# Asking for the first groups' places, features and B rows inside the first stage of a graph layer

## The chip, the cores and the metric

The kernel runs on one core of one Trainium2 chip. The metric is device time in microseconds (us). A core has TensorE (PE, with its weight loads shown apart as PEld), VectorE (DVE), ScalarE (ACT), GpSimd (POOL) and SyncE (SP). In this kernel SP computes nothing: it issues most of the DMAs, in the order of the program, and POOL issues the indirect DMAs that gather rows. Each engine has its own list of instructions and works through it in order.

## The reference

One layer of a graph network with a pre-norm and a gated update. There are N = 12,500 nodes with 128 features and E = 400,000 edges with 32 features, sorted by their destination.

```
h   = relu(layernorm(x))                                   # 12500 x 128
m   = relu(concat(h[src], h[dst], ea) @ w1 + b1) @ w2 + b2 # one row per edge
agg = segment_sum(m, dst)                                  # 12500 x 128
gi  = agg @ w_ih + b_ih ;  gh = h @ w_hh + b_hh            # three parts each: r, z, n
r = sigmoid(gi_r + gh_r) ; z = sigmoid(gi_z + gh_z) ; n = tanh(gi_n + r * gh_n)
out = x + (1 - z) * n + z * h
```

## The kernel before

w1 is cut into three parts. The part for the source gives a table A = h @ w1a, the part for the destination a table B = h @ w1b + b1, and both tables lie in the chip's memory (DRAM) with one row of 512 bytes for each node. The part for the edge features is applied with each group of edges.

**First stage** (lines 354 to 488). The nodes are taken in 14 batches (0 to 13): batch 0 has 4 tiles of 128 nodes, batches 1 to 11 have 8, batch 12 has 5, and batch 13 has the last 84 nodes. A loop over q = 0 to 28 works on chunks of up to 4 tiles, so most batches are two chunks. For each chunk ACT normalises (line 263), PE turns the tiles (line 450), DVE or ACT copies the turned tiles into hT_all, which stays in on-chip memory (line 468), PE multiplies them with w1a (line 487), and ACT copies the product into a buffer asb (line 458). When a batch is complete, SP stores asb to A (line 482). There are two asb buffers: batch b + 2 may be written into asb only when the store of batch b has landed. In the same loop SP asks for the later batches of x (line 375), for three rows of source numbers per q from q = 4 on (line 423, tile `at`, 60 rows in all), and stores the first three pieces of B (lines 258 and 260). Meanwhile POOL gathers the rows of x for edge groups 0 to 8.

**Edges** (from line 490 on). The edges form 391 groups of 8 tiles of 128 edges (group 0 has 5 tiles), and the loop at line 1075 takes half a group at a time (u = 0 to 781). A group needs:

- L, a tile of 128 rows. The lower 64 rows take the places of the edges' destinations (a row of whole numbers, repeated over 32 partitions for each half) and DVE turns these into a one-hot matrix in place (onehot_T, line 586). The upper 64 rows are the edge features. `fetch(q)` (line 567) asks for L for groups 2q and 2q + 1: two DMAs of 256 KB on SP, one from dstP (line 574) and one from eaP (line 577). There are three L buffers.
- RW, 40 rows of B around the group's destinations in two overlapping windows of 32, with the edge part of w1 below them. `window_rows(k)` (line 600) asks for the windows of group k: two DMAs of 16 KB on SP at an address that SP has read into a register. At the first group of a block of 14, SP loads the block's 14 addresses with one instruction (line 606). There are four RW buffers.
- the rows of the sources. Groups 0 to 8 gather x itself (before A exists), normalise it and multiply it with w1a. Sixty groups are brought by hand: 28 by ACT and 27 by DVE, which copy columns of hT_all, and 5 by SP, which issues one small DMA per row of A. The other 322 groups are gathered from A by POOL (line 163), eight indirect DMAs for each group and 2,576 in all, into a ring of 11 buffers G.

PE multiplies L with RW (line 683), the result and the gathered rows are added and rectified into RB (DVE line 713, or ACT line 725 for the raw and the turned groups), and PE sums RB over destinations with a second one-hot matrix (line 739). Every 14 groups a block of 512 nodes goes through the gated update (`node`, line 790), and the last block through `last_node` (line 857).

The DVE and ACT groups brought by hand are collected in buffers HE_dve and HE_act, two of each, from a pool `pj` that is open from the start. The L buffers belong to a pool `p3` that is opened when the first stage's pool is closed and takes its place in memory. Before the loop over the groups, after the first stage, SP's list holds `dst_tile(1)` (line 1033), `fetch(0)` to `fetch(2)`, and `window_rows(0)` to `window_rows(3)`. Inside the loop come `window_rows(k + 4)` and `fetch(k // 2 + 3)`.

In the built program, SP's DMAs (other than the single rows of the five SP groups) take eight completion semaphores in turn, and each of them waits until the DMA that had its semaphore before, the eighth before it, has landed.

Of the kernel before, what the change touches and what calls it, by code (L numbers as in the profile page):

```python
# [9 lines left out]
F32 = mybir.dt.float32  # L10
F16 = mybir.dt.float16
I32 = mybir.dt.int32
U8 = mybir.dt.uint8
U16 = mybir.dt.uint16
BF16 = mybir.dt.bfloat16
ET = mybir.EngineType
# [4 lines left out]
N, E, D, DE = 12500, 400000, 128, 32  # L21
# [5 lines left out]
NP = T // PAIR + 1  # L27
NU = 2 * NP

V = 32  # L30
SHIFT = 8
# [32 lines left out]
def tile_gnn(ctx: ExitStack, tc: tile.TileContext, x, src, srcT, dstT, dstP, eaT, eaP, w1, b1, w2T, b2,  # L64
# [238 lines left out]
    def setup(pool):  # L303
# [45 lines left out]
        yield  # L349
        place(0)  # L350

    st_all = const.tile([128, NT, 2], F32, name="st_all")
    nc.vector.memset(st_all[:, NFULL, :], 0.0)
    with tc.tile_pool(name="pp", bufs=3) as pp:
        bats = [(sum(BAT[:b]), n) for b, n in enumerate(BAT)]
        xs = {}

        def PB(b):
            return 128 if bats[b][0] < NFULL else N - NFULL * 128

        def nodes(t, i0, n, P):
            return t[i0 * 128:i0 * 128 + n * P, :].rearrange("(p i) f -> p i f", p=P)


        def columns(b, c, e):
            i0, n = bats[b]
            t = hT_all[:, i0 * 128:i0 * 128 + n * PB(b)].rearrange("f (p i) -> f i p", i=n)
            return t[:, c:e, :]

        def load(b):  # L370
            if b < len(bats):
                i0, n = bats[b]
                P = PB(b)
                xs[b] = pp.tile([128, 8, D], F32, name="xs", bufs=5)
                nc.sync.dma_start(xs[b][:P, :n, :], nodes(x, i0, n, P))

        mvs, asb = {}, {}

        def stat(b):
            if b < len(bats):  # L380
                i0, n = bats[b]
                mvs[b] = bn(pp, lambda j: xs[b][:PB(b), j, :], PB(b), n)

        def sqr(b):
            if b < len(bats):
                mvs[b] = bn_sqrt(pp, mvs[b], PB(b), bats[b][1])

        def fin(b):
            if b < len(bats):
                i0, n = bats[b]  # L390
                bn_fin(pp, st_all[:, i0:i0 + n, :], mvs.pop(b), PB(b), n)

        for b in range(5):
            load(b)
        w1b = const.tile([128, D], F32, name="w1b")
        nc.sync.dma_start(w1b, w1[128:256, :])
        wih_s = const.tile([128, 3 * D], F32, name="wih_s")
        nc.sync.dma_start(wih_s, wih)
        whh_s = const.tile([128, 3 * D], F32, name="whh_s")
        nc.sync.dma_start(whh_s, whh)  # L400
        w2T_s = const.tile([128, D], F32, name="w2T_s")
        nc.sync.dma_start(w2T_s, w2T)
        b2_s = const.tile([128, 1], F32, name="b2_s")
        nc.sync.dma_start(b2_s, b2.rearrange("(f o) -> f o", o=1))
        row = lambda v: v.rearrange("(o f) -> o f", o=1)
        nc.sync.dma_start(brow[32:33, 0:384], row(bih))
        nc.sync.dma_start(brow[32:33, 384:512], row(bhh)[:, 256:384])
        nc.sync.dma_start(brow[33:34, 0:256], row(bhh)[:, 0:256])
        nc.sync.dma_start(b1b, row(b1).to_broadcast([128, D]))
        for r in RW:  # L410
            for a in range(2):
                nc.sync.dma_start(r[64 + 32 * a:96 + 32 * a, a, :], w1[256:288, :])

        indices(1)
        nc.sync.dma_start(base_d, dstT[0:1, SUP0::PAIR])
        dst_tile(0)
        rows_left = list(range(NJ))

        def at_row():
            if rows_left:  # L420
                r = rows_left.pop(0)
                t0 = tiles(by_hand[r])[0]
                nc.sync.dma_start(at[r:r + 1, :], row(src[t0 * 128:(t0 + PAIR) * 128]))

        stat(0)
        sqr(0)
        fin(0)
        stat(1)
        sqr(1)
        chunks = [(b, c) for b, (i0, n) in enumerate(bats) for c in range(0, n, 4)]  # L430

        def chunk(q):
            b, c = chunks[q]
            i0, n = bats[b]
            return b, i0, c, min(n, c + 4), PB(b), (i0 + c) * 128

        pts, pas = {}, {}
        NC = len(chunks)
        setting = setup(pp)
        for q in range(NC + 3):  # L440
            if q < NC:
                b, i0, c, e, P, n0 = chunk(q)
                if c == 0:
                    stat(b + 2)
                    fin(b + 1)
            if 1 <= q <= NC:
                b, i0, c, e, P, n0 = chunk(q - 1)
                pts[q - 1] = SEGB[q % 2]
                for j in range(c, e):
                    nc.tensor.transpose(pts[q - 1][:, (j - c) * P:(j - c + 1) * P],  # L450
                                        xs[b][:P, j, :], ident[:P, :P])
                if e == bats[b][1]:
                    load(b + 5)
            if q >= 3:
                b, i0, c, e, P, n0 = chunk(q - 3)
                if c == 0:
                    asb[b] = pp.tile([128, 8, D], F32, name="asb", bufs=2)
                nc.scalar.copy(asb[b][:P, c:e, :], pas.pop(q - 3)[:P, :e - c, :])
            if q < NC:
                b, i0, c, e, P, n0 = chunk(q)  # L460
                for j in range(c, e):
                    relu_norm(xs[b][:P, j, :], xs[b][:P, j, :], st_all[:P, i0 + j, :])
                if e == bats[b][1]:
                    sqr(b + 2)
            if 1 <= q <= NC:
                b, i0, c, e, P, n0 = chunk(q - 1)
                copy = nc.scalar.copy if q % 4 == 0 else nc.vector.tensor_copy
                copy(columns(b, c, e), pts.pop(q - 1)[:, :(e - c) * P].rearrange(
                    "f (i p) -> f i p", i=e - c))
            if q >= 4:  # L470
                for _ in range(3):
                    at_row()
            if q >= 6:
                next(setting, None)
            if q in (6, 8, 10):
                batch_product(q // 2 - 3, pp, "bt", 1)
            if q in (7, 9, 11):
                batch_store(q // 2 - 3)
            if q >= 3:
                b, i0, c, e, P, n0 = chunk(q - 3)  # L480
                if e == bats[b][1]:
                    nc.sync.dma_start(nodes(A, i0, e, P), asb[b][:P, :e, :])
            if 2 <= q <= NC + 1:
                b, i0, c, e, P, n0 = chunk(q - 2)
                pas[q - 2] = ps2.tile([128, PAIR, D], F32, name="pre")
                for j in range(c, e):
                    nc.tensor.matmul(pas[q - 2][:P, j - c, :], columns(b, j, j + 1)[:, 0, :],
                                     w1a, start=True, stop=True)
# [72 lines left out]
        nc.vector.tensor_copy(flag, f[:, 6:7])  # L561


    Ls, OH, RT, HE, SEG = ({} for _ in range(5))
    hand = {}

    def fetch(q):
        if q * QP >= NP:
            return
        n = min(QP, NP - q * QP)  # L570
        c = slice(q * QP * 512, (q * QP + n) * 512)
        Ls[q] = p3.tile([128, QP * 512], F32, name="L")
        p = dstP[:, c]
        nc.sync.dma_start(
            Ls[q].bitcast(I32)[:2 * V, :n * 512],
            bass.AP(tensor=p.tensor, offset=p.offset, ap=[list(p.ap[0]), [0, V], [1, n * 512]]))
        nc.sync.dma_start(Ls[q][2 * V:, :n * 512], eaP[:, c])

    def onehot_T(k):
        if k >= NP:  # L580
# [8 lines left out]
                                    accum_out=dlast[:2 * V, n:n + 1])  # L589


    bases = {}

    def block(k):
        return max(b for b in range(NB) if BLOCKS[b][0] <= k)

    def slot(b, i):
        return i // 2 if b < NB - 1 else (BP - BLOCKS[b][1]) // 2 + i // 2

    def window_rows(k):  # L600
        if k >= NP:
            return
        b = block(k)
        k0, n, _ = BLOCKS[b]
        if k == k0:
            _, vals = nc.values_load_multi_w_load_instructions(
                base_i[0:1, b, 0:n], engines=[ET.SP], min_val=0, max_val=4 * D * LAST,
                skip_runtime_bounds_check_because="clamped above")
            for i, v in enumerate(vals):
                bases[k + i] = v  # L610
        v = bases.pop(k)
        for a in range(2):
            nc.sync.dma_start(RW[k % 4].bitcast(U8)[V * a:V * (a + 1), a, :],
                              B_bytes[bass.ds(v + 4 * D * SHIFT * a, 4 * D * V)].rearrange(
                                  "(p f) -> p f", p=V))

    def onehot(k):
        if k >= NP or (k % 2 and k > 1):
# [412 lines left out]

    gathers(0)
    dst_tile(1)
    for q in range(3):
        fetch(q)
    for k in range(4):
        window_rows(k)


    def stages(u):  # L1040
# [248 lines left out]
```

## Time and profile before

| what | value |
|---|---|
| median of 3 runs | 3385.01 us (3376.61 to 3388.27) |
| the profiled execution | 3383.87 us |
| its span, first to last instruction | 3382.1 us |
| PE, DVE, ACT, POOL busy | 71%, 65%, 91%, 75% of the span |
| mean granted TensorE clock | 0.795 |

Busy time leaves out what an engine spends on issuing: POOL is shown busy for about 0.94 us of each gather and idle for the 0.30 us that it takes to go on to the next. In the timeline a row gives start, duration, engine, line, operation, what is written and read, how many instructions were merged (x3), and in brackets the idle time before the first and what ended it. SPq is SP's queue: a row is the time of issuing, not of the transfer. When several rows of SP are merged, the duration runs from the first issue to the end of the last and holds the waits between them. What ended a wait is inferred from semaphores. Since the semaphores of DMAs are used in turn, the DMA named can be a later user of the same semaphore.

### The profile page before, as it was taken

Reading aid. Unit: us, or ns where it says so; the run is one execution under the profiler, and the core shown is the slowest. Engines: PE = TensorE matmul, PEld = TensorE weight load, DVE = VectorE, ACT = ScalarE, POOL = GpSimd, SP = SyncE. Lnnn points to the kernel's source line nnn. Section 1 sums busy time; section 2 is a strip of 40 time slices with the busy share of each in tenths; the row PEclk is TensorE's granted clock in tenths of the full one; section 3 lists DMA queues with packets and bytes.
Section 4 is the critical chain, followed back from the end, with each engine's and each line's share of the span. In section 5 each row is a group of like instructions: output and inputs, shape, how many; then the busy total and the mean of one; then the engine's idle time right before and its main releaser. Section 6 shows DMA issues by size and latency. Waiting matters only on the chain. (4 is left out here: it accounts for less than half of the span.)

```text
span 3382.1 us, 93395 instructions
## 1 busy us (share of the span) xinstructions
PE 2400.4 (71%) x13113; PEld 1554.8 (46%) x13113; DVE 2213.6 (65%) x16274; ACT 3081.1 (91%) x29057; POOL 2542.8 (75%) x2654
## 2 busy tenths in 40 slices
PE   7567766776677677668776777677667767766767
PEld 6444444444444444445444444444444444444445
DVE  8566666766666666666667766666656666666665
ACT  7599899999999998998999999999889998988975
POOL 7777777777777777777777777777777777777775
PEclk9778777887888777877877878787777787778778
DMA  6433444444444444444444444444444444343332
GB/s 215 104 92 84 95 99 101 99 97 103 96 95 99 97 98 95 99 104 97 96 98 97 98 95 105 97 99 98 95 98 96 100 95 99 94 96 94 92 94 67
DMA packets 196737, 335.77 MB, mean 99 GB/s; under 512 B 69445, under 2 KB 118148, under 8 KB 196112
## 3 DMA queue, kind: packets, MB, share of 16 engines
q0 software_dynamic: 84640, 173.51, 23.0%
q1 hardware_dynamic: 111327, 156.18, 17.8%
q14 instruction: 517, 4.23, 0.4%
q8 instruction: 109, 1.79, 0.2%
q10 hardware_dynamic: 144, 0.07, 0.0%
HBM read 309.25 MB, written 20.24 MB: 97 GB/s over the span
## 5 line engine op out<-in xcount | busy, mean ns | idle before, releaser
L163 POOL DMA_INDIRECT G<-A,src_i x2576 | 2475.8, 961 | 790.4 <-issue 761.2
L979 ACT COPY HE_act<-hT_all 128x4 uint8 x28672 | 2889.0, 189 | 52.9 <-issue 29.1
L986 DVE SCALAR_TENSOR_TENSOR both<-hT_all 128x4 uint16 x13824 | 1174.3, 154 | 930.3 <-issue 925.6
L683 PE MATMUL pre<-RW,L 128*128 128x256 f32 x3128 | 1136.1, 489 | 461.3 <-DMA RW<-B 237.7
L683 PEld LDWEIGHTS pre<-RW,L 128*128 128x128 f32 x3128 | 662.8, 237 | 736.8 <-issue 420.2
L739 PE MATMUL seg<-RB,OH 128*32 128x129 f32 x6250 | 592.7, 319 | 244.2 <-DVE RB L713 211.9
L739 PEld LDWEIGHTS seg<-RB,OH 128*32 128x32 f32 x6250 | 328.0, 123 | 590.7 <-DVE RB L713 310.1
L713 DVE CUSTOM_DVE_ANT_0 RB<-pre,G 128x1024 f32<-128x1024 f32 x323 | 391.1, 1211 | 70.9 <-DMA G<-A,src_i 56.5
L586 DVE TENSOR_SCALAR L<-L,node_of 64x512 f32<-64x512 int32 x382 | 185.9, 487 | 62.2 <-DMA L<-in_dstP 59.9
L725 ACT ACTIVATE RB<-pre 128x1024 f32<-128x1024 f32 x64 | 65.0, 1016 | 91.0 <-PE pre L694 91.0
L633 DVE TENSOR_TENSOR OH<-dloc,seg 128x512 f32<-128x512 f16 (+1 forms) x198 | 132.3, 669 | 0.0
L765 PE MATMUL nd<-spot,sums 128*128 128x40 f32 x782 | 119.6, 326 | 3.6 <-DVE sums L748 3.6
L765 PEld LDWEIGHTS nd<-spot,sums 128*128 128x128 f32 x782 | 115.5, 237 | 12.7 <-issue 8.8
L991 DVE COPY HE_dve<-both 128x512 uint8<-128x512 uint8 x216 | 97.6, 452 | 7.4
L244 PE MATMUL nd<-w1b,hT_all 128*128 128x128 f32 x224 | 49.4, 368 | 73.1 <-DVE xb L850 73.1
L734 PE MATMUL seg<-zrow 1*128 1x129 bf16 x196 | 45.5, 232 | 78.1 <-DVE OH L633 78.0
L694 PEld LDWEIGHTS pre<-w1a,HE_dve 128*128 128x128 f32 x432 | 89.1, 255 | 12.4
L694 PEld LDWEIGHTS pre<-w1a,HE_act 128*128 128x128 f32 x448 | 85.9, 238 | 11.0
L694 PE MATMUL pre<-w1a,HE_dve 128*128 128x128 f32 x432 | 85.4, 333 | 0.0
L694 PE MATMUL pre<-w1a,HE_act 128*128 128x128 f32 x448 | 83.7, 319 | 0.0
L163 POOL DMA_INDIRECT G<-in_x,src_i x69 | 65.6, 950 | 21.9 <-issue 20.7
L244 PEld LDWEIGHTS nd<-w1b,hT_all 128*128 128x128 f32 x224 | 35.2, 231 | 85.5 <-DVE xb L850 80.0
(177 smaller groups left out, 1346.2 us busy)
## 6 DMA issues: line engine op xcount, KB each, us to landing
G_sp<-A SPq DMA_DIRECT2D x5120, 0.5 KB
L<-in_dstP SPq DMA_DIRECT2D x195, 256.0 KB
L<-in_eaP SPq DMA_DIRECT2D x195, 256.0 KB
G<-A,src_i POOLq DMA_INDIRECT x2576, 2.5
RW<-B SPq DMA_DIRECT2D x782, 16.0 KB
xb<-in_x SPq DMA_DIRECT2D x26, 256.0 KB
out<-xb SPq DMA_DIRECT2D x26, 256.0 KB
xs<-in_x SPq DMA_DIRECT2D x11, 512.0 KB
```

The lines of the kernel that those rows point to most:

```text
L163: fetched = nc.gpsimd.indirect_dma_start(out=G[k][:, j, a, :], out_offset=None, in_=table, in_offset=bass.IndirectOffsetOnAxis(ap=src_i[c] ...
L244: nc.tensor.matmul(pm[:m, i:i + D], hT_all[:, n0 + i:n0 + i + m], w1b, start=True, stop=True)
L586: nc.vector.tensor_scalar(o, i, node_of[:, k:k + 1], None, op0=ALU.is_equal)
L633: nc.vector.tensor_tensor(p, dloc[:, e0:e1, None].to_broadcast(shape), row[:, None, :].to_broadcast(shape), op=ALU.is_equal)
L683: nc.tensor.matmul(p[:, 2 * i:2 * i + 2, :], Ls[k // QP][:, c0:c0 + 128], RW[k % 4], start=True, stop=not raw)
L694: nc.tensor.matmul(p[:, 2 * i + a, :], cols, w1a, start=False, stop=n + 1 == len(l) or l[n + 1][1] != j)
L713: made = nc.vector._custom_dve(TENSOR_ADD_SAT, out=o, in0=p, in1=G[k].rearrange("p j a f -> p (j a) f")[:, c, :], s0=float("inf"), s1=0.0)
L739: nc.tensor.matmul(p[r0:r0 + V, :D + 1], OH[k][:, a * GRP + j, :], RB[k % 2][:, 2 * j + a, :D + 1], start=False, stop=all(b != a for _, _, ...
L765: nc.tensor.matmul(p[:, bass.ds(offs[i], V + SHIFT)], sums[:, slot(b, i), :D], spot[:, i % 2, :], start=False, stop=i == len(offs) - 1)
L979: nc.scalar.copy(he[:, e * 4:e * 4 + 4], column(v))
L986: nc.vector.scalar_tensor_tensor(both[:, (e0 % PIECE + i) // 2, :], column(vals[i + 1]), 256.0, column(vals[i]), op0=ALU.mult, op1=ALU.add)
L991: nc.vector.tensor_copy(he[:, p0 * 4:(p0 + PIECE) * 4].rearrange("p (n c b) -> p n c b", c=2, b=4), both.bitcast(U8).rearrange("p n (b c) ...
```

## The change

`fetch` and `window_rows` are defined before the first stage, and their first calls are moved into it. The addresses and the windows of groups 0 to 3 are asked for at q = 16, and L for groups 0 and 1, 2 and 3, 4 and 5 at q = 18, 20 and 22. The first three L tiles no longer come from the pool `p3` but are the first HE_dve, the second HE_dve and the first HE_act buffer. The functions are otherwise the same, and the calls after the first stage are gone. The loop over groups is not changed, so its `fetch(3)`, `fetch(4)` and `fetch(5)` now take L buffers that nobody has used before.

```diff
+    Ls = {}
+
+    def fetch(q):
+        if q * QP >= NP:
+            return
+        n = min(QP, NP - q * QP)
+        c = slice(q * QP * 512, (q * QP + n) * 512)
+        if q < 3:
+            Ls[q] = pj.tile([128, QP * 512], F32, name="HE_dve" if q < 2 else "HE_act")
+        else:
+            Ls[q] = p3.tile([128, QP * 512], F32, name="L")
+        p = dstP[:, c]
+        nc.sync.dma_start(
+            Ls[q].bitcast(I32)[:2 * V, :n * 512],
+            bass.AP(tensor=p.tensor, offset=p.offset, ap=[list(p.ap[0]), [0, V], [1, n * 512]]))
+        nc.sync.dma_start(Ls[q][2 * V:, :n * 512], eaP[:, c])
...
+    def window_rows(k):
...
+        if k == k0:
+            _, vals = nc.values_load_multi_w_load_instructions(
+                base_i[0:1, b, 0:n], engines=[ET.SP], min_val=0, max_val=4 * D * LAST,
+                skip_runtime_bounds_check_because="clamped above")
...
+        for a in range(2):
+            nc.sync.dma_start(RW[k % 4].bitcast(U8)[V * a:V * (a + 1), a, :],
...
@@ -476,6 +515,11 @@
                 batch_product(q // 2 - 3, pp, "bt", 1)
             if q in (7, 9, 11):
                 batch_store(q // 2 - 3)
+            if q == 16:
+                for k in range(4):
+                    window_rows(k)
+            if q in (18, 20, 22):
+                fetch((18, 20, 22).index(q))
             if q >= 3:
                 b, i0, c, e, P, n0 = chunk(q - 3)
                 if e == bats[b][1]:
...
     gathers(0)
     dst_tile(1)
-    for q in range(3):
-        fetch(q)
-    for k in range(4):
-        window_rows(k)
```

More of the change, by code (lines that the diff above doesn't have):

```diff
@@ L350, in setup, with block @@
         place(0)
+    Ls = {}
[13 more added lines that the diff above has]
+        nc.sync.dma_start(Ls[q][2 * V:, :n * 512], eaP[:, c])
+    bases = {}
+    def block(k):
+        return max(b for b in range(NB) if BLOCKS[b][0] <= k)
+    def window_rows(k):
+        if k >= NP:
+            return
+        b = block(k)
+        k0, n, _ = BLOCKS[b]
+        if k == k0:
+            _, vals = nc.values_load_multi_w_load_instructions(
+                base_i[0:1, b, 0:n], engines=[ET.SP], min_val=0, max_val=4 * D * LAST,
+                skip_runtime_bounds_check_because="clamped above")
+            for i, v in enumerate(vals):
+                bases[k + i] = v
+        v = bases.pop(k)
+        for a in range(2):
+            nc.sync.dma_start(RW[k % 4].bitcast(U8)[V * a:V * (a + 1), a, :],
+                              B_bytes[bass.ds(v + 4 * D * SHIFT * a, 4 * D * V)].rearrange(
+                                  "(p f) -> p f", p=V))
     st_all = const.tile([128, NT, 2], F32, name="st_all")
@@ L561, in check_windows @@
         nc.vector.tensor_copy(flag, f[:, 6:7])
-    Ls, OH, RT, HE, SEG = ({} for _ in range(5))
+    OH, RT, HE, SEG = ({} for _ in range(4))
     hand = {}
[L567 to L577, printed above, removed]
     def onehot_T(k):
@@ L589, in onehot_T @@
                                     accum_out=dlast[:2 * V, n:n + 1])
-    bases = {}
-    def block(k):
-        return max(b for b in range(NB) if BLOCKS[b][0] <= k)
     def slot(b, i):
         return i // 2 if b < NB - 1 else (BP - BLOCKS[b][1]) // 2 + i // 2
[L600 to L615, printed above, removed]
     def onehot(k):
```

## The prediction

> **What bounds the kernel now.** I read the page first, then what POOL waited for, then the timeline of POOL, then what DVE waited for in three stretches, then the first 130 us queue by queue. By busy time ACT looks like the bound, but the groups show that POOL is:
>
> ```profile
> span 3382.1 us, 93395 instructions
> L163 POOL DMA_INDIRECT G<-A,src_i x2576 | 2475.8, 961 | 790.4 <-issue 761.2
> ```
>
> The waits of POOL from 93 us to the end, and its timeline at the start of the A gathers, at its one later stop, and at its last gather:
>
> ```profile
> POOL G L163 <- issue: 761.2, 2496, 0.3
> POOL G L163 <- PE misc L666: 3.3, 4, 2.3
> ...
> 88.71 0.94 POOL L163 DMA_INDIRECT G<-in_x,src_i  x1 [0.30 <-issue]
> 92.84 0.94 POOL L163 DMA_INDIRECT G<-A,src_i  x1 [3.18 <-DMA L<-in_dstP]
> ...
> 121.57 0.94 POOL L163 DMA_INDIRECT G<-A,src_i  x1 [0.30 <-issue]
> 124.86 0.94 POOL L163 DMA_INDIRECT G<-A,src_i  x1 [2.34 <-PE misc L666]
> ...
> 3354.97 0.94 POOL L163 DMA_INDIRECT G<-A,src_i  x1 [0.30 <-issue]
> ```
>
> From 92.84 to 3354.97 POOL issues one gather after another. The only real stop is 2.34 us at 124.86, for a G buffer that a raw group still held. All else is the 0.3 us behind every gather. Whether the rest of the kernel has to follow POOL is told by the addition that uses the gathered rows (DVE, line 713), asked from 0 to 2250 us and from 2250 to 3225 us:
>
> ```profile
> L713 DVE CUSTOM_DVE_ANT_0 RB<-pre,G x212: 1204/1212/1226, 203.6 to 2249.2; 128x1024 f32<-128x1024 f32 x106
>   PE pre L683: 7.9, 8
> ...
> L713 DVE CUSTOM_DVE_ANT_0 RB<-pre,G x97: 1204/1217/1226, 2249.2 to 3220.2; 128x1024 f32<-128x1024 f32 x97
>   DMA G<-A,src_i: 56.5, 27
> ```
>
> The first use comes at 203.6, 111 us after POOL's first A gather. Up to 2249 the addition never waits for rows: ACT, DVE and PE start late and catch up. From there to 3220 it waits 27 times for rows that have only just been asked for. So the end follows POOL: the start of the A gathers, 2,576 gathers, and the last groups (3354.97 to 3382.1). Time saved for ACT, DVE or PE in the first 2200 us only makes them catch up sooner, while time lost by POOL is lost for good.
>
> **What the change aims at.** DVE and PE at the seam of the two stages:
>
> ```profile
> 91.14 1.10 PE L666 MATMUL misc<-ident,G 128*128 128x128 f32 x3 [2.44 <-ACT G L263]
> 100.32 0.48 DVE L586 TENSOR_SCALAR L<-L,node_of 64x512 f32<-64x512 int32 x1 [9.76 <-DMA L<-in_dstP]
> 118.39 1.19 PE L683 MATMUL pre<-RW,L 128*128 128x256 f32 x2 [11.73 <-DMA RW<-B]
> ```
>
> DVE stands 9.76 us for L, and the first product comes at 118.39, though the first raw tiles were turned by 92.24. Both waits go. But by the paragraph above, this is worth only what POOL gains: its stop at 124.86 falls away, since that buffer will be free earlier. That is 2.34 less the usual 0.30, or 2.04 us.
>
> **What the moved DMAs displace.** SP's queue from q = 16 on, as it stands before:
>
> ```profile
> 62.76 0.87 SPq L423 DMA_DIRECT2D at<-in_src  x3
> 66.01 0.32 SPq L375 DMA_DIRECT2D xs<-in_x  x1
> 66.37 0.85 SPq L423 DMA_DIRECT2D at<-in_src  x3
> 67.31 0.37 SPq L482 DMA_DIRECT2D A<-asb  x1
> ...
> 76.86 0.37 SPq L482 DMA_DIRECT2D A<-asb  x1
> ...
> 81.62 8.06 SPq L482 DMA_DIRECT2D A<-asb  x4
> ...
> 90.21 0.66 SPq L574 DMA_DIRECT2D L<-in_dstP  x1
> ...
> 91.65 0.57 SPq L574 DMA_DIRECT2D L<-in_dstP  x1
> ...
> 93.02 0.55 SPq L574 DMA_DIRECT2D L<-in_dstP  x1
> ...
> 93.61 4.96 SPq L577 DMA_DIRECT2D L<-in_eaP  x1
> ...
> 100.40 1.86 SPq L613 DMA_DIRECT2D RW<-B  x4
> ```
>
> The stores of batches 7 and 9 are issued at 67.31 and 76.86, and the row of four is batches 10 to 13. POOL's first A gather needs all of them landed: the last issue ends at 89.68 and the gather starts at 92.84, 3.2 us later. Now an L fetch, its landing and what stands behind it:
>
> ```profile
> SPq L613 <- DMA L<-in_dstP: 13.5, 2, 7.7
> ...
> 108.22 0.32 SPq L613 DMA_DIRECT2D RW<-B  x1
> ...
> 116.75 0.32 SPq L613 DMA_DIRECT2D RW<-B  x1
> ...
> 303.75 0.58 SPq L574 DMA_DIRECT2D L<-in_dstP  x1
> ...
> 312.81 0.33 SPq L507 DMA_DIRECT2D stats<-st_all  x1
> ```
>
> The windows issued at 108.22 and 116.75 are the eighth DMAs after the fetches of 91.65 and 93.02, so these are the landings of the second and third places tile. The first landed by 100.32, when DVE's wait ended. One after the other they take 10.1, 7.9 and 8.5 us. A lone fetch of 303.75 held up its eighth successor until 312.81, so it took 9.1 us. And the first windows, issued at 100.40, end PE's wait only at 118.39: they landed when the third L did, some 18 us after their issue. So an L fetch is slow, the fetches follow one another, and a DMA behind them in SP's queue is complete only after them.
>
> The Trainium skill, page "DMA: Bandwidth & Descriptors", section "Anatomy of one DMA", fits a DMA issued by GpSimd with 2.0 us plus its bytes over 436,000 per us; carried over to 256 KB that is an estimate of 2.6 us, nothing on SP would be held up, and the sum would be the gain of 2.04 us alone, 3381.8 us. The trace's 9 to 10 us speak against it. Section "Rules for kernel authors" of that page says that an outermost dimension of size c confines a DMA to at most c engines; the places fetch has an outermost dimension of 2, so by that rule the A stores too, which need all engines, wait behind it.
>
> I take 10.5 us from the issue of a places DMA to the landing of its pair: 10.1, and some for the eaP half, issued behind it. SP's list in the new order, step by step:
>
> - q = 16. The three rows end at 63.63. The load of the 14 addresses takes 1.8 us (98.57, the end of the row at 93.61, to 100.40), and eight windows at 0.46 us (four in 1.86) take 3.7. The load of x goes out at 69.2 instead of 66.01, and the store of batch 7 at 70.4 instead of 67.31. Three more rows end at 71.4, and the wait for that load of x to land makes it 71.8: first L fetch.
> - q = 20. The third row of `at` has the semaphore of the first places DMA, the second fetch has those of the first pair. SP stands until 71.8 + 10.5 = 82.3. The second pair goes out there, then three rows, and the store of batch 9 at about 84.7 instead of 76.86.
> - q = 22. The same again: the third fetch goes out at 82.3 + 10.5 = 92.8, and the store of batch 10 at about 95.2 instead of 81.62. It is complete only after the third L, at 103.6.
>
> With only two asb buffers ACT may copy batch 12 only when batch 10 has landed:
>
> ```profile
> 83.41 0.59 ACT L458 COPY asb<-pre 128x512 f32<-128x512 f32 x1 [0.26 <-ACT xs L263]
> ...
> 87.62 0.77 ACT L458 COPY asb<-pre 128x512 f32<-128x512 f32 x2 [0.94 <-ACT xs L263]
> ...
> 89.05 0.26 ACT L458 COPY asb<-pre 84x128 f32<-84x128 f32 x1 [0.66 <-DMA A<-asb]
> ```
>
> The copy at 87.62 moves to 103.6, by 16.0 us. The last copies and stores behind it take as long as before, so POOL's first A gather moves from 92.84 to 108.8. ACT's earlier stands (batch 11's copy, 83.41, waits for batch 9) lie inside these 16.0.
>
> **Edits that cost nothing.** HE_dve and HE_act: the first two DVE groups are brought from u = 14 on, when L for groups 0 to 3 has long been used; ACT's first group takes the other HE_act buffer. fetch(3) to fetch(5) find free buffers, which spares SP short stands that only ACT, DVE and PE would feel. The load of x moved to 69.2 is used several us later; were it late, it would add at most its own 3.2 us.
>
> **The sum.** +16.0 for POOL's start, -2.04 for its stop: +14.0 on the profiled 3383.87 us is 3397.9. This execution stands 1.1 us below the median of 3385.01, so against the median the sum is 3399, and that is what I predict. The times of the bounds and rivals are on the profiled execution.
>
> Bounds of the unknown terms. The trace shows loads held behind an L fetch, but no row shows a store held. If a store lands 3.2 us after its issue whatever is ahead, batch 10's lands at 95.6 + 3.2 = 98.8, the copy moves by 11.2 and the sum is +9.2: 3393. I take the held value, since the windows are the nearest row. With 7.9 us per fetch instead of 10.5 the third L is in 7.8 earlier: +6.2, 3390. Traffic of the first stage could slow the fetches: with 13 us each, +7.5, 3405.
>
> **Rivals.**
>
> A. Not slower but faster: ACT, DVE and PE set the end. Then the first product moves from 118.39 to about 94.5, as the tiles were turned by 92.24, and nearly all of the 24 us arrives: about 3361. For it speaks ACT's 91%. Against it stand the 56.5 us in which the addition waits for rows after 2249. It needs 20 us of slack between POOL and the rest, and from 2249 to 3220 there is none.
>
> B. The fetches fit into the first stage and the A stores are not delayed. Only the 2.04 us are gained: 3382. For it: SP has free time between the rows above. Against it: 10 us per fetch and eight semaphores.
>
> C. Only SP's stands count and stores are not held: 3393, as worked out.
>
> D. The seam is worse: fetches of 13 us, or source rows late behind them: 3405 or more. For it: gathers of x and A stores share the time. Against it: the fetch at 303.75 ran beside gathers as well, in 9.1 us.
>
> **How the numbers follow.** Chances: forecast 0.66, A 0.04, B 0.10, C 0.12, D 0.08. The three runs spread by 12 us and their median moves by some 4, so about 0.3% (10.2 us) is what can be told from no change. The forecast lies 3.8 us beyond that and ends slower 0.56, within 0.10. C ends slower 0.04 and within 0.08, B within 0.09 and faster 0.01, D slower 0.08, A faster 0.04. Together: faster 0.05, same 0.27, slower 0.68. The range 3386 to 3408 holds nearly all of the forecast and C and the lower part of D; the likeliest case's own range is 3391 to 3405.
>
> **What would show it.** POOL's first A gather near 109 instead of 92.84, and idle before it some 19 us. SP's rows: L fetches near 72, 82 and 93, waits of SP for L inside the first stage, and A stores of batches 9 and 10 near 85 and 95. ACT waiting for A stores to land, 15 us or more in all. No DVE wait of 9.76 for L, no PE wait of 11.73 for RW, no 2.34 at POOL. The additions waiting for rows earlier than 2249. The prediction is wrong if POOL's first A gather stays before 96, or if it moves and the end does not.

## The result, and the profile after

The changed kernel takes 3396.66 us (median of 9 runs, 3394.01 to 3402.00); the kernel before, run beside it, 3382.74 us (9 runs, 3376.61 to 3388.27). The ratio is 1.0042, with a 95% interval of 1.0034 to 1.0051: slower by 13.9 us. The profiled execution after took 3400.03 us at a granted clock of 0.79, that of before 3383.87 us at 0.795. Lines of code below the change stand 10 to 50 lines further down: the source rows are line 462, the A store line 526, the two DMAs of an L fetch lines 364 and 367, the windows line 387, ACT's copy into asb line 497, the addition line 723.

The page after, and the group of POOL's gathers from A:

```profile
span 3398.3 us, 93394 instructions
...
L163 POOL DMA_INDIRECT G<-A,src_i x2576 | 2478.8, 962 | 804.0 <-issue 765.7 <-DMA A<-asb 18.5 <-DVE both L996 7.0
```

POOL's timeline after, at the start of the A gathers, at the place of the former stop, and at the last gather:

```profile
88.83 0.95 POOL L163 DMA_INDIRECT G<-in_x,src_i  x1 [0.30 <-issue]
108.25 0.95 POOL L163 DMA_INDIRECT G<-A,src_i  x1 [18.47 <-DMA A<-asb]
109.50 0.94 POOL L163 DMA_INDIRECT G<-A,src_i  x1 [0.30 <-issue]
...
125.84 0.94 POOL L163 DMA_INDIRECT G<-A,src_i  x1 [0.31 <-issue]
...
3371.60 0.94 POOL L163 DMA_INDIRECT G<-A,src_i  x1 [0.30 <-issue]
```

The first A gather comes at 108.25 instead of 92.84 (+15.41), after an idle stretch of 18.47 us that ends when a store to A has landed. From there POOL runs through without a stop until 3371.60 (before 3354.97): 3263.35 us, 1.22 more than before. From the last gather to the end of the span it is 26.70 us instead of 27.13. 15.41 + 1.22 - 0.43 is the 16.2 us between the two spans.

SP's queue after, and SP's waits for L's DMAs inside the first stage:

```profile
63.02 1.52 SPq L462 DMA_DIRECT2D at<-in_src  x3
66.30 3.72 SPq L387 DMA_DIRECT2D RW<-B  x8
...
71.51 0.37 SPq L526 DMA_DIRECT2D A<-asb  x1
...
72.89 0.67 SPq L364 DMA_DIRECT2D HE_dve<-in_dstP  x1
...
75.33 0.37 SPq L526 DMA_DIRECT2D A<-asb  x1
75.74 6.80 SPq L462 DMA_DIRECT2D at<-in_src  x3
83.14 0.58 SPq L364 DMA_DIRECT2D HE_dve<-in_dstP  x1
...
85.42 0.37 SPq L526 DMA_DIRECT2D A<-asb  x1
85.83 7.04 SPq L462 DMA_DIRECT2D at<-in_src  x3
93.27 0.57 SPq L364 DMA_DIRECT2D HE_act<-in_dstP  x1
...
95.53 10.82 SPq L526 DMA_DIRECT2D A<-asb  x4
```
```profile
SPq L462 <- DMA HE_dve<-in_dstP: 11.9, 2, 6.0
```

The three rows of source numbers that took 0.9 us take 6.80 and 7.04 us: in each of them SP stands for the semaphore of an L fetch, 11.9 us in two waits. The stores of batches 9 and 10 go out at 85.42 and 95.53 instead of 76.86 and 81.62. ACT's copies into asb after:

```profile
75.00 0.59 ACT L497 COPY asb<-pre 128x512 f32<-128x512 f32 x1 [1.38 <-DMA A<-asb]
...
85.11 0.59 ACT L497 COPY asb<-pre 128x512 f32<-128x512 f32 x1 [4.86 <-DMA A<-asb]
...
95.28 0.59 ACT L497 COPY asb<-pre 128x512 f32<-128x512 f32 x1 [5.83 <-DMA A<-asb]
...
104.32 0.75 ACT L497 COPY asb<-pre 128x512 f32<-128x512 f32 x2 [6.30 <-DMA A<-asb]
105.72 0.26 ACT L497 COPY asb<-pre 84x128 f32<-84x128 f32 x1 [0.64 <-PE pre L531]
```

ACT waits four times for a store to land, 18.4 us in all (0.7 before), and the copy of batch 12 stands at 104.32 instead of 87.62. How a store is late shows in the trace's 16 completion records of an A store of eight tiles (a places DMA has only 3 records in the form used here). In us after the issue:

```
kernel  DMA                          issued   first  middle  last
before  A store                       76.86    2.9    3.1     3.2
after   places half of L (3 records)  83.14    1.0    8.8     9.5
after   A store behind it             85.42    2.7    3.4     9.8
```

Fourteen of this store's 16 records come within 3.6 us of its issue, nearly as before. Only two are late, at 8.4 and 9.8 us, and the last of them, at 95.18, comes 1.9 us after the pair of the fetch ahead has landed (93.25). ACT needs all 16. The stores behind the other two fetches look the same: 14 records within 3.3 us, two after 8.3 to 9.7.

Whether the rest follows POOL, by the addition's waits after, from 1700 to 2250 us and from 2250 to 3240 us:

```profile
L723 DVE CUSTOM_DVE_ANT_0 RB<-pre,G x56: 1204/1214/1225, 1702.6 to 2240.5; 128x1024 f32<-128x1024 f32 x56
  DMA G<-A,src_i: 7.3, 4
...
L723 DVE CUSTOM_DVE_ANT_0 RB<-pre,G x98: 1205/1216/1226, 2252.1 to 3236.6; 128x1024 f32<-128x1024 f32 x98
  DMA G<-A,src_i: 61.9, 27
```

Before, the first wait for rows came after 2249. Now four come earlier. The others have caught up with POOL sooner, as is to be expected when POOL is later. At the seam itself PE gained little:

```profile
107.81 1.24 PE L676 MATMUL misc<-ident,G 128*128 128x128 f32 x3 [2.13 <-ACT G L263]
...
113.29 1.06 PE L693 MATMUL pre<-RW,HE_dve 128*128 128x256 f32 x2
```

Its first product is at 113.29 instead of 118.39. It no longer waits for windows or L, but the raw tiles that it turns come from ACT, and ACT stands for the stores.

### The profile page after: what moved, and what is told of

Its sections match the earlier page's. It is cut to its first block, busy times and chain, and to the rows that moved or that the text cites. A ratio compares the mean times of both kernels' runs of the same rounds, so it can differ in the third digit from the quotient of the medians.

```text
span 3398.3 us, 93394 instructions
## 1 busy us (share of the span) xinstructions
PE 2397.7 (71%) x13113; PEld 1553.5 (46%) x13113; DVE 2215.7 (65%) x16274; ACT 3081.4 (91%) x29057; POOL 2546.0 (75%) x2654
## 5 line engine op out<-in xcount | busy, mean ns | idle before, releaser
L163 POOL DMA_INDIRECT G<-A,src_i x2576 | 2478.8, 962 | 804.0 <-issue 765.7
L989 ACT COPY HE_act<-hT_all 128x4 uint8 x28672 | 2889.5, 189 | 51.8 <-issue 27.6
L996 DVE SCALAR_TENSOR_TENSOR both<-hT_all 128x4 uint16 x13824 | 1173.8, 153 | 933.3 <-issue 928.8
L693 PE MATMUL pre<-RW,L 128*128 128x256 f32 x3080 | 1113.3, 488 | 439.7 <-DVE RB L723 234.4
L693 PEld LDWEIGHTS pre<-RW,L 128*128 128x128 f32 x3080 | 651.6, 236 | 712.6 <-issue 397.8
```

The source lines that it names most:

```text
L163: fetched = nc.gpsimd.indirect_dma_start(out=G[k][:, j, a, :], out_offset=None, in_=table, in_offset=bass.IndirectOffsetOnAxis(ap=src_i[c] ...
L693: nc.tensor.matmul(p[:, 2 * i:2 * i + 2, :], Ls[k // QP][:, c0:c0 + 128], RW[k % 4], start=True, stop=not raw)
L989: nc.scalar.copy(he[:, e * 4:e * 4 + 4], column(v))
L996: nc.vector.scalar_tensor_tensor(both[:, (e0 % PIECE + i) // 2, :], column(vals[i + 1]), 256.0, column(vals[i]), op0=ALU.mult, op1=ALU.add)
```

## The experiments

The theory: the three L fetches, each some 10 us long, delay the stores to A and with them POOL's start, and POOL's lateness is the end's. The rivals: the address load and the windows on SP's queue do it; the bytes, or SP's longer list, do it and not the form of the fetches; the end does not follow POOL.

On the chips of all runs below, the kernel before itself takes 5,692 to 5,739 us, so a time expected on the scale of 3,383 us is missed there, and only differences on the same chip and rows of the trace are held against the expectations. What differs shows in the waits of the kernel before with split fetches (line, what it waited for, us in total, times, longest):

```profile
POOL G L163 <- DVE RB L715: 2148.8, 219, 44.0
ACT HE_act L981 <- issue: 2145.7, 3079, 1.9
DVE both L988 <- issue: 1657.1, 1681, 2.6
```

ACT stands 2,146 us between small copies for nothing that the profile shows (27.6 us in the profile after), DVE 1,657 us (928.8 there), and POOL waits 2,149 us for buffers: on these chips POOL isn't the bound.

**One part alone.** Windows alone moved into the first stage (the fetches go back to where they were), and fetches alone moved:

```diff
 e3_windows_only, against the changed kernel
-            if q in (18, 20, 22):
-                fetch((18, 20, 22).index(q))
...
+    for q in range(3):
+        fetch(q)
```
```diff
 e4_fetch_only, against the changed kernel
-            if q == 16:
-                for k in range(4):
-                    window_rows(k)
...
+    for k in range(4):
+        window_rows(k)
```

> One part of the change alone: the addresses and the windows of groups 0 to 3 at q = 16, the three L fetches after the first stage as before (but into the HE buffers). Theory (the L fetches delay the stores, the windows only shift SP by some 4 us): POOL's first A gather at 93 to 95 us, its stop at 124.86 gone or smaller, time 3380 to 3387. Rival (the address load and the windows on SP's queue are what delays the stores): first A gather at 103 or later, time over 3391.

> The other part alone: L fetches at q = 18, 20 and 22, addresses and windows after the first stage. Theory: the first fetch goes out some 4 us sooner than with the windows ahead of it (near 69 instead of 72.9), SP stands for each fetch as in the changed kernel, the third fetch is out near 89 and lands near 99, POOL's first A gather at 103 to 106 us, time 3390 to 3396. Rival (the windows): POOL's first A gather at 93 to 96 and the time near 3383.

POOL's first A gather with the windows alone:

```profile
168.35 0.94 POOL L163 DMA_INDIRECT G<-A,src_i  x1 [78.94 <-DMA HE_dve<-in_dstP]
```

and with the fetches alone, with SP's queue there and SP's wait:

```profile
177.67 0.95 POOL L163 DMA_INDIRECT G<-A,src_i  x1 [88.11 <-DMA A<-asb]
```
```profile
143.97 0.65 SPq L364 DMA_DIRECT2D HE_dve<-in_dstP  x1
...
153.53 0.59 SPq L364 DMA_DIRECT2D HE_dve<-in_dstP  x1
...
163.20 0.57 SPq L364 DMA_DIRECT2D HE_act<-in_dstP  x1
...
165.46 10.31 SPq L523 DMA_DIRECT2D A<-asb  x4
```
```profile
SPq L462 <- DMA HE_dve<-in_dstP: 11.0, 2, 5.6
```

The fetches alone start POOL 9.3 us later than the windows alone, with 9.6 us between fetches, 11.0 us in which SP stands for them and a row of four stores of over 10 us, much as in the profile after. Against the kernels with nothing moved on such chips, in which POOL starts at 166.43 to 167.27 (rows and text below), the windows alone cost 1.1 to 1.9 us and the fetches alone 10.4 to 11.2. The whole change costs 15.3 to 15.6 there. So the fetches are what starts POOL late, and the windows alone do little. But the two do not simply add up: with the address load and the windows ahead of them on SP's queue, the fetches go out some 4.5 us later (the first at 148.50 in the slow-POOL kernel after, at 143.97 here), and so does what waits for them. The times say nothing here: 5738.10 us with the fetches alone (ratio to before 0.9996, 0.9982 to 1.0010) and 5735.22 with the windows alone (0.9986, 0.9970 to 1.0003). Where POOL waits for buffers, a late POOL costs nothing that can be told.

**The form of the fetch.** The places half of each fetch is asked for as two DMAs, each one row of places repeated over 32 partitions, in the changed kernel and in the kernel before. The bytes are the same, and SP issues one DMA more for each fetch.

```diff
 e1_after_split, e1b_after_split (the same kernel on another chip); e2_before_split alike
-        nc.sync.dma_start(
-            Ls[q].bitcast(I32)[:2 * V, :n * 512],
-            bass.AP(tensor=p.tensor, offset=p.offset, ap=[list(p.ap[0]), [0, V], [1, n * 512]]))
+        for a in range(2):
+            r = dstP[a:a + 1, c]
+            nc.sync.dma_start(
+                Ls[q].bitcast(I32)[V * a:V * a + V, :n * 512],
+                bass.AP(tensor=r.tensor, offset=r.offset, ap=[[0, V], [1, n * 512]]))
```

> The changed kernel, with the places half of every L fetch issued as two DMAs of 32 rows, one for each half of the group, so that the row that is repeated 32 times is the outermost dimension and the data is spread over more than two DMA engines. Theory (a places DMA is slow because two engines carry it, it holds SP by the eight semaphores and holds the A stores behind it): a fetch lands in 3 to 5 us, SP no longer stands at q = 20 and 22, ACT waits under 2 us for A stores, POOL's first A gather is at 93 to 96 us instead of 108.2, and the time is 3380 to 3387 us. Rival (the 1.5 MB of the fetches are too much for the DMA engines beside the stores and gathers of the first stage, however they are spread): POOL's first A gather stays at 104 to 109 and the time near 3395.

> The kernel before, with the same split of the places half of every L fetch and nothing moved. Theory (the end follows POOL, and ACT, DVE and PE only catch up sooner): L and the windows land some 15 us sooner at the seam, PE's first product is near 100 to 104 us instead of 118.4, POOL's first A gather stays at 93, its stop of 2.34 us goes, and the time is 3379 to 3385 us, that is 0 to 4 us less than before. Rival (ACT, DVE and PE set the end): the 15 us arrive, about 3368.

> The changed kernel with the places half of every L fetch split into two DMAs of 32 rows, once more, since in the first call every kernel, the one before included, took some 5730 us, with ACT and SP standing for their instructions and POOL waiting 2149 us for buffers, so that POOL was not the bound there. Theory, where the kernel before takes some 3383 us: a fetch lands in 3 to 5 us, SP does not stand at q = 20 and 22, ACT waits under 2 us for A stores, POOL's first A gather is at 93 to 96 us instead of 108.2, time 3380 to 3387. Rival (too many bytes for the DMA engines in the first stage): first A gather at 104 to 109, time near 3395.

The changed kernel with split fetches, on the second chip:

```profile
168.32 0.94 POOL L163 DMA_INDIRECT G<-A,src_i  x1 [79.03 <-DMA dst_i<-in_dstT]
```
```profile
148.53 0.78 SPq L366 DMA_DIRECT2D HE_dve<-in_dstP  x2
...
152.96 0.78 SPq L366 DMA_DIRECT2D HE_dve<-in_dstP  x2
...
157.52 0.78 SPq L366 DMA_DIRECT2D HE_act<-in_dstP  x2
...
160.05 6.17 SPq L528 DMA_DIRECT2D A<-asb  x4
```

The fetches go out 4.5 us apart, and POOL starts at 168.32 (169.17 on the first chip; the kernel before with split fetches 166.43). Of the delay no more than 2 or 3 us is left, with all fetches and windows still inside the first stage. SP stands only 0.5 to 0.6 us for a DMA of a fetch there, and ACT 1.9 to 2.3 us in all for stores. In the kernel before with split fetches the first product comes 9.5 us after POOL's first A gather (175.93) instead of 25.6, with nothing moved; POOL's wait for a buffer of a raw group, which was expected to go, does not go on such a chip (27.0 us in four waits). In time, split fetches give 0.9976 of the kernel before (0.9960 to 0.9993) and 0.9985 (0.9968 to 1.0002) in the changed kernel, and 0.9981 (0.9970 to 0.9993) in the kernel before: a gain of some 0.2% that the kernel before has as well, so it doesn't come from the move.

**Fewer instructions.** To make POOL the bound again, the 60 groups brought by hand were made cheap: one copy of fixed columns for each ACT and DVE group and eight DMAs for each SP group, so that the rows of these groups are not the right ones. Beside the kernels before and after in this form ran one with 96 POOL instructions ahead of the first A gather, and one with 52 ACT copies at the seam.

```diff
 t1_thin_before, t2_thin_after
+            (nc.scalar.copy if m == "act" else nc.vector.tensor_copy)(hand[k], hT_all[:, :PAIR * 128])
+            return
...
+                fetched = nc.sync.dma_start(G[k][:, j, a, :], A[0:128, :])
```
```diff
 t3_thin_pool; t4_thin_act has 52 times nc.scalar.copy(idle, idle), 128 x 256, at the same place
+    for _ in range(96):
+        nc.gpsimd.iota(idle, pattern=[[1, 32]], base=0, channel_multiplier=0, ...)
```

> The kernel before, with most of the work by hand left out: an ACT or DVE group is filled with one copy of the first 1024 columns of hT_all instead of 1024 or 576 small copies, and an SP group with eight DMAs of the first 128 rows of A instead of 1024 of one row, so its values are not those of the reference. All 2,576 gathers of POOL, all matmuls and all additions stay. This takes away the 28,672 and 13,824 small instructions for which ACT and DVE stood in the calls that took 5,730 us. Theory: POOL becomes the bound again: 2,576 gathers at 1.266 us after the first A gather and some 25 to 60 us behind them, that is about 3290 to 3330 us after the first A gather, wherever that comes (93 us in the first runs, 166 in the later ones): 3385 or about 3460 to 3490. Rival (ACT or PE still set the end): POOL waits for buffers for more than 100 us and the time is far longer.

> The changed kernel with the same work left out. Theory: POOL's first A gather 10 to 16 us later than in the thin kernel before, and the time later by the same, less up to 2 us: +9 to +15 us, and ACT and DVE, which have hardly any work by hand, change nothing in it. Rival (the delay came in by ACT, DVE or PE being late for their work by hand): the two thin kernels take the same time.

> The thin kernel before, with 96 small iotas on POOL ahead of the first A gather, some 15 us of POOL's time, and nothing else. Theory (what POOL loses is lost for good): the first A gather comes later by what the iotas take beyond the wait for A, 12 to 20 us, and the time by the same amount within 3 us. Rival: the end moves by less than half of it.

> The thin kernel before, with 52 small copies on ACT ahead of the first group, some 15 us in which the raw groups' normalisation, and with it PE and DVE, must wait, while POOL's list is as before. Theory (ACT, DVE and PE only catch up): POOL's first A gather is not moved, its stop for the buffer of a raw group grows by at most some 15 us less what RW and L held up anyway (5 us or less), and the time moves by 0 to 6 us. Rival (the seam counts for all engines): the time moves by 12 us or more, as with POOL.

| kernel | median us | runs from, to | first A gather |
|---|---|---|---|
| thin, before | 4384.87 | 4381.84 to 4393.26 | 167.27 |
| thin, after | 4395.75 | 4372.89 to 4400.68 | 182.59 |
| thin, before, 96 POOL instructions | 4383.51 | 4376.29 to 4395.88 | 167.27 |
| thin, before, 52 ACT copies | 4381.66 | 4377.75 to 4388.45 | 166.46 |

This settles nothing on the end. The thin kernel before was expected to take some 3,460 to 3,490 us with POOL as the bound. The medians of the first two differ by 10.9 us, but their runs overlap, and POOL still waits for buffers in both (here the thin kernel before):

```profile
POOL G L163 <- DVE RB L713: 794.3, 105, 22.1
```

The third kernel missed its aim: its POOL instructions ran inside POOL's idle stretch ahead of the first A gather, which did not move. The fourth agrees with the prediction, in which ACT's time at the seam is worth nothing, but POOL wasn't the bound there. What the four do show is that POOL's start moves by 15.3 us, as in the profile after, also at this speed.

**A slower POOL.** The other way round: two more POOL instructions behind each gather from A, which write to a scratch tile that nobody reads. POOL then needs about 2.35 us for each gather (6055.5 us from the first of the 2,576 to the last, in the rows below).

```diff
 p1_slow_pool_before, p2_slow_pool_after, p3_slow_pool_after_split (with the split of e1)
+    idle = const.tile([128, 512], F32, name="idle")
...
+                if k >= RAW:
+                    for _ in range(2):
+                        nc.gpsimd.iota(idle, pattern=[[1, 512]], base=0, channel_multiplier=0, ...)
```

> The kernel before, with two more instructions of POOL (a row of 512 whole numbers written into a scratch tile) behind each of the 2,576 gathers from A; nothing else is changed. At about 0.6 us each they make POOL's work some 2.5 us per gather, so 6,300 to 6,700 us in all where the kernel before takes 5,730 us on such a chip. Theory: POOL is then the bound again, as it was in the profile of before: its waits for buffers, 2,149 us with the fetches alone, fall below 50 us, and the addition of the DVE groups waits for rows through the whole run. First A gather near 167, as in the kernel before on such a chip. Rival (the end does not follow POOL): POOL still waits hundreds of us for buffers.

> The changed kernel with the same two instructions behind each gather. Theory: POOL's first A gather comes some 15 us later than in the slow-POOL kernel before (about 182 against 167) and POOL never catches up, so the time is 12 to 18 us longer. Rival (the end does not follow POOL's start): within 4 us of it.

> The changed kernel with the same two instructions behind each gather, and the places half of each L fetch asked for as two DMAs, each of one row of places repeated over 32 partitions (the outermost dimension is then 32 and not 2); the bytes are the same. Theory (the form of the fetch delays the stores, not its bytes or its place): POOL's first A gather is back near 168, and the time is within 4 us of the slow-POOL kernel before. Rival (the bytes or the place in the first stage delay the stores): first A gather near 182 and 12 to 18 us longer, as with the changed kernel.

| kernel | median us | runs from, to | ratio to the kernel before |
|---|---|---|---|
| slow POOL, before | 6245.33 | 6243.60 to 6245.60 | 1.0964 (1.0921 to 1.1007) |
| slow POOL, after | 6259.38 | 6258.47 to 6269.27 | 1.0989 (1.0946 to 1.1033) |
| slow POOL, after, split fetches | 6245.72 | 6243.07 to 6246.85 | 1.0964 (1.0921 to 1.1007) |

POOL's two largest waits in total, and then its first and last gather, in the slow-POOL kernel before and after, and the two gathers after with split fetches:

```profile
POOL G L165 <- issue: 430.2, 2639, 0.6
POOL G L165 <- DMA L<-in_dstP: 77.8, 1, 77.8
```
```profile
167.05 0.94 POOL L165 DMA_INDIRECT G<-A,src_i  x1 [77.83 <-DMA L<-in_dstP]
...
6222.59 0.96 POOL L165 DMA_INDIRECT G<-A,src_i  x1 [0.15 <-issue]
```
```profile
POOL G L165 <- issue: 429.9, 2634, 0.6
POOL G L165 <- DMA A<-asb: 93.2, 1, 93.2
```
```profile
182.67 0.94 POOL L165 DMA_INDIRECT G<-A,src_i  x1 [93.23 <-DMA A<-asb]
...
6246.38 0.96 POOL L165 DMA_INDIRECT G<-A,src_i  x1 [0.15 <-issue]
```
```profile
167.96 0.94 POOL L165 DMA_INDIRECT G<-A,src_i  x1 [78.70 <-DMA dst_i<-in_dstT]
...
6224.38 0.96 POOL L165 DMA_INDIRECT G<-A,src_i  x1 [0.15 <-issue]
```

In none of the three does POOL wait longer than 0.3 us for a buffer, and the additions wait for rows through the whole run (in the slow-POOL kernel before 263 times, 2,339.6 us in all). So POOL is the bound, as was meant, if at slightly less than the 6,300 to 6,700 us expected. The start is 15.6 us later with the change, and the median 14.1 us longer (the profiled execution of the second row is the longest of its four, and 8.2 us of its last gather's 23.8 come from the pace and not from the start); the runs of the two kernels do not overlap. With split fetches the start is back to within 0.9 us and the median to within 0.4 us. So where POOL is the bound, its late start is paid nearly in full. And neither the bytes nor the place nor SP's longer list is enough to make the change slow: with all three kept, the other form of the fetches takes the delay away. It takes both, the old form and a place ahead of the stores. The completions of the DMAs tell how:

```
kernel             DMA                                issued   first  middle  last
slow, after        places half of L (3 records)       158.70    1.0    8.1     8.6
slow, after        A store behind it                  161.03    2.5    3.5     8.5
slow, after split  places, first 32 rows (16 records) 152.00    1.9    2.2     2.7
slow, after split  places, other 32 rows (16 records) 152.37    2.1    2.4     2.7
slow, after split  A store behind it                  154.47    2.5    2.7     3.5
```

Spread over all 16 records the places of this fetch land within 2.7 us of their issue, and the store behind them is nearly as quick as those of the slow-POOL kernel before (2.9 us).

## Why the prediction was right

Predicted were 3399 us, 14.0 us over the profiled execution; the medians differ by 13.9. The mechanism is borne out step by step below, but that the two numbers agree to 0.1 us is luck. Term by term the profiles give 15.41 for the start where 16.0 were expected, and +1.22 for POOL's stretch of gathers where -2.04 were; with the 0.43 us less behind the last gather that is 16.2. The profiled execution after stands 3.4 us above its median and that of before 1.1, which brings the 16.2 down to 13.9.

**The bound.** That time lost by POOL is lost for good is what the profile after shows from end to end (the sum of the first section), and what the slow-POOL kernels show as an effect. Their POOL is slower, so for the kernel as it is, at 1.27 us for each gather, the claim rests on its profiles. A rival that the prediction does not name is that ACT's loss makes the end later, since ACT, busy for 91%, stands 18.4 us for the stores. The trace settles it: from its second A gather on POOL waits for nobody longer than 0.3 us, so no other engine sets when its last gather comes, and the end is 26.70 us behind that gather where it was 27.13 before.

**SP's list.** The fetches were expected at 71.8, 82.3 and 92.8 and went out at 72.89, 83.14 and 93.27. 0.9 us of the first one's lateness lies in the three rows at 63.02, which start 0.26 us later than before and take 1.52 us instead of 0.87. A fetch took 10.2, 10.1 and 9.8 us from its issue to the landing of its pair, not 10.5. The two errors nearly cancel: the third pair landed at 103.07, where 92.8 + 10.5 = 103.3 was expected. But the store behind it landed only 1.15 us after the pair, at 104.22, where the prediction allowed 0.3, so the copy of batch 12 moved by 16.7 us instead of 16.0.

**The held stores.** This was the open term: 9.2 us in all if the stores weren't held, 14.0 if they were. They are held: the stores of batches 8, 9 and 10 land 9.7, 9.8 and 8.7 us after their issue, so rival C falls. The section "Rules for kernel authors" of the page "DMA: Bandwidth & Descriptors" of the Trainium skill says that an outermost dimension of a size c below 16 confines a DMA to at most c engines, which are two here. The two late records of 16 in each store behind a fetch agree with that. Why a places DMA itself has 3 records and not 2 no run shows. The section's advice, to put a dimension outermost whose size is a multiple of 16, is what the split does. The section "Queues, rings and completion order" has each DMA engine take its descriptors in ring order; by that only the store's parts on the engines of the fetch should be late. This too agrees with 14 records within 3.6 us and two after 8.3 to 9.8. The estimate of 2.6 us from that page's "Anatomy of one DMA" is far below the 9.2 to 9.5 us in which the places of the three fetches land as they are, and near the 2.6 to 3.1 us of the split ones.

**The edits taken as free.** They were. The load of x went out at 70.12, and between 60 and 110 us no computing engine waits for a load of x, nor for an L fetch; the 9.76 us of DVE and the 11.73 us of PE are gone too.

**The last copies and stores.** "As long as before" was off by 1.3 us: from batch 12's copy to the first A gather it took 3.93 us instead of 5.22, mostly because the store of batch 13 landed 1.5 us after its issue instead of 2.6. So POOL's start moved by 15.41 us where 16.0 were expected.

**The stop at 124.86.** It is gone, and without the wait for the first A gather (18.47 and 3.18) POOL's idle time ahead of its A gathers fell by 1.7 us, from 787.2 to 785.5. But the gathers were busy for 2478.8 us instead of 2475.8, 1.2 ns more each, so the stretch from the first to the last grew by 1.22 us instead of shrinking. Why the gathers took 1.2 ns more stays open, and differences of this size lie within the spread of the runs.

**Rivals.** A needed the first product near 94.5; it came at 113.29. PE's last wait ahead of it is for a raw tile that ACT normalises, and ACT stands behind the late stores, which the rival had not reckoned with. Its 94.5 also rested on a misreading: by 92.24 PE had turned three raw tiles, and the two that also stand ahead of the first product in its list came only at 106.01. That the product came 5 us sooner and the end 14 us later speaks against it either way. B needed stores that keep their time; that is nearly what the split fetches do. D needed fetches of 13 us. Left open: how the changed kernel with split fetches stands to the kernel before where that takes 3,383 us. It was run only where both take some 5,700 us, and with a slowed POOL, where it neither gained nor lost.

## What to carry to other kernels

Look first for the engine whose lateness nobody can make up, and ask of a prefetch what it delays in that engine's chain, not only which waits it removes. A DMA that repeats a row is better written so that its outermost dimension is large: in the form with two, it held up the store behind it on its queue by 5 to 7 us here, and as two DMAs of 32 rows each by 0.5 to 1.4 us. When a chip moves the bound elsewhere, slow the resource in question until it bounds again, and then test.

## What the runs showed of the hardware

On the chips of the experiments the same kernel took 5,692 to 5,739 us instead of 3,383, with a granted clock of 0.67 instead of 0.795, and in the kernel before with split fetches ACT stood for 2,146 us with no wait that the profile shows, where it stood for 28 us in the profile after. The thin kernels, with 37,734 instructions instead of about 93,400, took 4,385 us on such a chip. No run took apart why.

A DMA that stands behind a fetch on the same queue is not held as a whole: in the profile after and the slow-POOL kernel after, 14 of the 16 parts of the store behind each fetch landed within 3.8 us of its issue, and two only after 7.5 to 9.8. And three fetches that follow each other directly land one after the other: in the kernel before the places landed 10.1, 16.6 and 23.7 us after their issue, and with the windows alone moved 11.4, 17.6 and 23.9.
